# Residual stack on one core: the last projection's sums move from GpSimd to VectorE and to adding DMAs, its products add up in the PSUM bank

## The chip, the core and the metric

One core of a Trainium2 chip runs the whole program. Its engines are TensorE (PE in the profile, with its weight loads as PEld), VectorE (DVE), ScalarE (ACT), GpSimd (POOL) and SyncE (SP), which issues DMAs. Sixteen DMA engines move data between DRAM and the on-chip memory. The metric is the device time of one execution in microseconds; lower is better.

## The reference, cut to what matters

There are four residual layers on `x`, of 64 x 32 rows (2048) by 512 columns:

```python
x = x + L0(x)    # per-batch 32 x 32 mixing of the rows of a batch
x = x + L1(x)    # 512 x 512 linear layer plus a rank-16 adapter
x = x + L2(x)    # attention with a paged cache: 32 query heads, 8 key heads, head size 128
x = x + L3(x)    # per-batch 32 x 32 mixing, as in L0, with other weights
```

What the change touches is the end of L2, and L3. The heads' outputs `o` (2048 x 4096) are multiplied by `Wo` (4096 x 512) and added to `x`; then L3 takes, for each batch of 32 rows, `out = x + W_b^T x`. Everything is 32-bit floating point.

## The kernel before, in words

**Stages.** The first three layers up to the attention fill most of the time. They write `x` after L1 into 16 DRAM tiles `x_dram[t]` of 128 rows, and the turned head outputs into `o_dram[g][t]`: for each tile t of 128 rows and each half g of the key heads, 128 x 16 x 128 numbers. The last stage (from L1483 on) multiplies `o` by `Wo`, adds, mixes and stores.

**Two levels of Strassen's scheme (in Winograd's form).** The rows are cut into four quads q of four tiles. One quad is a 2 x 2 block matrix: i chooses two of its tiles, j chooses the half g of the heads. `Wo` is likewise cut into 2 x 2 blocks: heads by columns `lo` and `hi`. Seven products, numbered 1 to 7, give the quad's four blocks of the result. Each of them is one `Outer(what, quad)`, and `TARGETS` (L1505) says into which result blocks its output goes: 14 additions of a 128 x 512 block for a quad. Within an Outer the same scheme is used again: operand tiles "11", "12", "21", "22" of 128 x 1024, sums s1 to s4 of them, and seven products p of eight 128 x 128 x 128 matmuls each (`ORDER`, L290). I call one such product a **step**. `Outer.multiply` (L342) issues its matmuls into a bank of PSUM, `Outer.post` (L358) reads the bank.

**What an Outer costs each engine before.** The operand tiles come from `o_dram` by SP's DMAs into a ring of 12 tiles of 512 KB (`ring_tile`, L280; `load`, L309; `release`, L322). VectorE makes s1 to s4 (L340). For Outers 7, 5, 6 and 3 the operands are themselves sums of blocks: `combine` (L1575) makes them, on VectorE for 7, 6 and the first 5, on GpSimd for the others. Each product has a bank of its own out of six; ScalarE copies the first into `u` (L362), and VectorE adds the later ones to it and to one another: seven adds from a bank for an Outer (L367 to L380). The result `m` of 128 x 512 is then added by GpSimd into `acc` (L1519), which holds the rows of a quad on chip; `acc` has two buffers, so quads are loaded (L1499) and stored (L1503) between their two rounds.

**The weights' sums.** For each of the seven numbers, `weight_sum` (L246) makes four sums of blocks of `Wo`, in two halves of 128 x 512 each (L251). Before, in the last stage, GpSimd makes those for 2 (the fourth), 7, 4, 6 and 3, VectorE those for 5. `first_weights` (L1559) and `second_weights` (L1563) are VectorE's.

**L3.** `fetch_mix` (L1521) gathers 32 weights for each row by an indirect DMA from GpSimd, `make_diag` (L1526) spreads them on VectorE into a block-diagonal 128 x 128 matrix, and `mixed` (L1536) multiplies it with the rows on TensorE, adds the product to the rows on VectorE (L1544) and may send the part out; `store_out` (L1548) sends a tile.

**Order.** Everything in this stage is issued in an order written out by hand; each engine works through its own queue in that order. Outers 1 of quads 0 and 1 have been made during the end of the attention, from GpSimd's loads. `order` (L1590) then has 26 Outers: first round 2, 2, 7, 7, 4, 4 of quads 0 and 1, and 1, 7, 2, 4 of quads 2 and 3; second round 5, 6, 3 of quads 3, 0, 1, 2. The loop at L1726 takes steps 0 to 181. After each step's matmuls and its `post` come releases, then what `then(step, ...)` has put under this step, then `pump` (L1583), which issues waiting loads of `o` on SP as far as ring tiles are free. So a number given to `then` decides both when work is issued and what it stands behind on its engine. An offset like `s - 4` is four steps before the Outer's first.

Of the kernel before, what the change touches and what calls it, by code (L numbers as in the profile page):

```python
# [77 lines left out]
def resid_kernel(  # L78
# [128 lines left out]
    x_dram = [dram.tile([P, HID], F32, name=f"x_{t}") for t in range(NT)]  # L207
# [38 lines left out]
    def weight_sum(what, name, engine):  # L246

        w = w_of[what]
        a, b = {1: ("3", "11"), 2: ("22", "1"), 3: ("22", "3"), 4: ("2", "21")}[name]
        for k in (0, 1):  # L250
            engine.tensor_tensor(w.part(str(name), k), w.part(a, k), w.part(b, k), ALU.subtract)  # L251
# [6 lines left out]
    def fourth_weights(k, i, engine):  # L258

        lo, hi = slice(0, HID // 2), slice(HID // 2, HID)  # L260
        dst = w_sb["o", KG + k][:, :, hi]
        if i == 0:
            engine.tensor_tensor(dst, w_sb["o", k][:, :, hi], w_sb["o", k][:, :, lo], ALU.add)
        else:
            engine.tensor_tensor(dst, dst, w_sb["o", KG + k][:, :, lo], ALU.subtract)
# [19 lines left out]
    class Outer:  # L285
# [13 lines left out]
        FROM = {1: (0, 0), 2: (0, 1), 4: (1, 1)}  # L299
        count = 0  # L300

        def __init__(self, what, quad):
            self.what, self.quad = what, quad
            self.m, self.tag = {}, {}
            self.n = Outer.count
            Outer.count += 1
            self.pair = 0 if self.n < 3 else self.n % 2

        def load(self, key, queue=nc.sync, block=None):  # L309
            i, j = block or self.FROM[self.what]  # L310
            a, b = int(key[0]) - 1, int(key[1]) - 1
            self.tag[key], self.m[key] = ring_tile()
            queue.dma_start(
                out=self.m[key],
                in_=o_dram[j][4 * self.quad + 2 * i + a][:, b * 2 * REP : (b + 1) * 2 * REP],
            )

        def adopt(self, key, other):

            self.tag[key], self.m[key] = other.tag.pop(key), other.m.pop(key)  # L320
# [33 lines left out]

        def block(self, a, h):
            return self.out[:, a, h * P : (h + 1) * P]

        def post(self, p):  # L358
# [20 lines left out]
            else:  # L379
                add(self.block(1, 0), self.u3, ps, ALU.subtract)  # L380
# [1102 lines left out]
    with ExitStack() as l3:  # L1483
# [10 lines left out]
        acc, diag, rows_of_mix = {}, {}, {}  # L1494

        def load_rows(q):
            acc[q] = pool.tile([P, 4, HID], F32, name="acc", bufs=2)
            for a in range(4):
                nc.sync.dma_start(out=acc[q][:, a], in_=x_dram[4 * q + a])  # L1499

        def store_rows(q):
            for a in range(4):
                nc.scalar.dma_start(out=x_dram[4 * q + a], in_=acc[q][:, a])  # L1503
# [11 lines left out]
        def accumulate(o, engine):  # L1515
            op = ALU.subtract if o.what == 4 else ALU.add
            for i, j in TARGETS[o.what]:
                part = acc[o.quad][:, 2 * i : 2 * i + 2, (lo, hi)[j]]
                engine.tensor_tensor(part, part, o.out, op)  # L1519

        def fetch_mix(q, a):  # L1521
            t = 4 * q + a
            rows_of_mix[t] = pool.tile([P, S], F32, name="mix_rows")
            gather(rows_of_mix[t], w3, cond_rows[:, t : t + 1])

        def make_diag(q, a):  # L1526
            t = 4 * q + a
            diag[t] = pool.tile([P, NB, S], F32, name="mix_diag", bufs=4)
            add(  # L1529
                diag[t],  # L1530
                rows_of_mix.pop(t).unsqueeze(1).to_broadcast([P, NB, S]),
# [4 lines left out]
        def mixed(q, a, cols, queue=nc.scalar):  # L1536
# [3 lines left out]
            part = acc[q][:, a, cols]  # L1540
# [3 lines left out]
            add(part, ps, part, ALU.add)  # L1544
# [3 lines left out]
        def store_out(q, a, queue=nc.scalar):  # L1548
            t = 4 * q + a
            queue.dma_start(out=out[t * P : (t + 1) * P, :], in_=acc[q][:, a])  # L1550
# [16 lines left out]
        class Operand:  # L1567


            load, release = Outer.load, Outer.release  # L1570

# [3 lines left out]
        def combine(dst, key, a, op, b, engine):  # L1575
            engine.tensor_tensor(dst.m[key], a.m[key], b.m[key], op)  # L1576
# [12 lines left out]
        with tc.manual_schedule(engines=ENGINES):  # L1589
            order = [(2, 0), (2, 1), (7, 0), (7, 1), (4, 0), (4, 1)]  # L1590
            order += [(w, q) for q in (2, 3) for w in (1, 7, 2, 4)]
            order += [(w, q) for q in (3, 0, 1, 2) for w in (5, 6, 3)]
# [3 lines left out]
            KEYS = ("21", "22", "11", "12")  # L1596

            for what, q in order[1:]:
                o, s = of[what, q], base[what, q]
                begin = {"s1": -2, "s2": -2, "s3": -1, "s4": 1}  # L1600
                if what in (1, 2, 4):
                    for key in ("11", "12", "21", "22"):
                        pending.append((o, key, None))
                if what == 7:
                    single = (1, q) not in of
                    a11 = Operand(q) if single else of[1, q]
                    for key in KEYS:
                        if single:
                            pending.append((a11, key, (0, 0)))
                        pending.append((o, key, (1, 0)))  # L1610
                    when = (-5, -4, -4, -3) if single else (-9, -6, -6, -9)
                    for key, w in zip(KEYS, when):
                        then(s + w, combine, o, key, a11, ALU.subtract, o, nc.vector)
                        if single:
                            then(s + w, a11.release, key)
                if what == 1:
                    begin["s3"] = 0
                if what == 5:
                    a22 = Operand(q)
                    for key in KEYS:  # L1620
                        pending.append((o, key, (1, 0)))
                        pending.append((a22, key, (1, 1)))
                    for key in ("21", "12", "11", "22"):
                        pending.append((of[6, q], key, (0, 0)))
                    for key in ("21", "12", "11", "22"):
                        pending.append((of[3, q], key, (0, 1)))
                    first = q == 3
                    engine = nc.vector if first else nc.gpsimd
                    for key, w in zip(KEYS, (-10, -8, -5, -4) if first else (-11, -9, -7, -5)):
                        then(s + w, combine, o, key, o, ALU.add, a22, engine)  # L1630
                        then(s + w, a22.release, key)
                    for key, w in zip(("21", "12", "11", "22"), (-1, -1, 1, 2)):
                        then(s + w, combine, of[6, q], key, o, ALU.subtract, of[6, q], nc.vector)
                    for key, w in zip(("21", "12", "11", "22"), (4, 5, 6, 7)):
                        then(s + w, combine, of[3, q], key, of[3, q], ALU.subtract, of[6, q], nc.gpsimd)
                    begin["s3"] = 0
                for name, w in begin.items():
                    then(s + w, o.sum, name, nc.vector)
                then(s + 6, accumulate, o, nc.gpsimd)
            then(6, accumulate, early[2], nc.gpsimd)  # L1640

            for w, what, name in (
                (0, 7, 1),
                (1, 7, 2),
                (3, 7, 4),
                (5, 7, 3),
                (9, 4, 1),
                (11, 4, 2),
                (13, 4, 4),
                (15, 4, 3),  # L1650
            ):
                then(w, weight_sum, what, name, nc.gpsimd)
            for q, w in ((0, 37), (1, 44), (2, 73)):
                then(w, store_rows, q)
            then(39, load_rows, 2)
            then(50, load_rows, 3)
# [4 lines left out]
            for k in range(KG):  # L1661
                then(s + 18, first_weights, k)
                then(s + 25, second_weights, k)
            for w, what, name in (
                (20, 5, 1),
                (21, 5, 2),
                (22, 5, 4),
                (26, 5, 3),
                (27, 6, 1),
                (28, 6, 2),  # L1670
                (29, 6, 4),
                (30, 6, 3),
                (33, 3, 1),
                (34, 3, 2),
                (36, 3, 4),
                (38, 3, 3),
            ):
                engine = nc.vector if what == 5 else nc.gpsimd
                then(s + w, weight_sum, what, name, engine)
            for q in (3, 0, 1, 2):  # L1680
                s = base[3, q]
                for a in range(4):
                    then(s - 14 + 3 * a, fetch_mix, q, a)
                    then(s - 12 + 3 * a, make_diag, q, a)
                if q != 2:
                    for a in range(4):
                        then(s + 10 + a, mixed, q, a, slice(0, HID), None)
                        then(s + 11 + a, store_out, q, a)
            for q, w in ((0, 80), (1, 130), (2, 151)):
                then(w, load_rows, q)  # L1690
            s = base[3, 2]
            todo[s + 6] = [x for x in todo[s + 6] if x[0] is not accumulate]
            then(s + 1, mixed, 2, 2, slice(0, HID), nc.sync)
            then(s + 2, mixed, 2, 3, slice(0, HID), nc.sync)
            then(s + 3, mixed, 2, 0, lo, nc.sync)
            then(s + 4, mixed, 2, 1, lo, nc.sync)
            last = outers[-1]

            def part_of_last(a, h):
                at = HID // 2 + h * P  # L1700
                return acc[2][:, a, at : at + P]

            def add_to_last(a, h, b):
                add(part_of_last(a, h), part_of_last(a, h), b, ALU.add)

            then(s + 2, lambda: add_to_last(0, 0, last.block(0, 0)))
            then(s + 3, lambda: add_to_last(1, 0, last.u3))
# [123 lines left out]
```

## Time and profile before

| | us |
|---|---|
| median of 3 runs (lowest, highest) | 2493.77 (2492.73, 2495.66) |
| the profiled execution, its own time | 2495.89 |
| its span in the trace | 2494.1 |
| busy in the span: PE, DVE, POOL, ACT | 2391.5, 1847.8, 1472.3, 1404.3 |
| last stage, PE's first product to the end of the span | 2056.6 to 2494.1 |
| POOL in the last stage: adds into acc, combinations | 101.4, 65.3 |

Lines of the profile name an engine, a line of the kernel, an operation, what it writes and reads, and a count. "<-" after an idle time names what ended it. One 128 x 128 x 128 matmul is recorded twice, so a step has 16 records. A window's line gives its length, then the busy time and records of each engine, the clock granted to TensorE, the busy share of the 16 DMA engines and what they moved in GB/s. Times of single instructions within the text are microseconds from the span's start.

### The profile page before, as it was taken

What the parts mean: (1) busy time and instruction counts of PE and PEld (TensorE: products, weight loads), DVE (VectorE), ACT (ScalarE), POOL (GpSimd) and SP (SyncE); (2) the same over time, 40 slices, a digit from 0 to 9 for tenths busy, and PEclk for the clock granted to TensorE, in tenths of its full rate; (3) what the DMA queues carried; (4) which work ended last, traced back from release to release, by engine and by line L of the source; (5) the groups of instructions that cost most, each with busy time, mean ns of one, the idle gap of its engine ahead of it and who ended that gap; (6) DMA issues with size and microseconds to landing.
All of it is one profiled execution on the core that took longest, in us unless ns stands there. A gap on an engine that the chain in (4) does not pass through costs nothing. (4 is left out here: it accounts for less than half of the span.)

```text
span 2494.1 us, 50604 instructions
## 1 busy us (share of the span) xinstructions
PE 2391.5 (96%) x15142; PEld 1896.7 (76%) x15142; DVE 1847.8 (74%) x3788; ACT 1404.3 (56%) x4024; POOL 1472.3 (59%) x1394
## 2 busy tenths in 40 slices
PE   8999999999999999999999999999999897996787
PEld 4657777777777777777777777777777797996787
DVE  5567777777777777887877777777777777668766
ACT  2347777777777777676777777777777650000000
POOL 3346565656566666665565666566566658226774
PEclk9999999999999999999999999999999999998999
DMA  8876767676667677766666666666578767774552
GB/s 274 259 228 183 207 183 208 184 202 190 196 191 203 188 229 238 214 187 183 180 175 194 175 192 173 194 177 188 174 220 249 226 197 288 240 275 140 168 210 83
DMA packets 485696, 502.66 MB, mean 202 GB/s; under 512 B 69952, under 2 KB 392768, under 8 KB 485424
## 3 DMA queue, kind: packets, MB, share of 16 engines
q1 hardware_dynamic: 425552, 311.00, 40.8%
q0 software_dynamic: 55600, 181.35, 24.7%
q10 hardware_dynamic: 4272, 7.08, 0.8%
q8 instruction: 122, 2.00, 0.3%
q14 instruction: 150, 1.23, 0.2%
HBM read 427.91 MB, written 79.69 MB: 204 GB/s over the span
## 5 line engine op out<-in xcount | busy, mean ns | idle before, releaser
L105 POOL DMA_INDIRECT v_sb<-v,v_rows x512 | 546.3, 1067 | 354.0 <-PE o_ps L1055 243.3
L1055 PE MATMUL o_ps<-pT,v_sb 128*128 128x128 f32 x4096 | 624.9, 275 | 1.1 <-ACT oT L1090 0.8
L1055 PEld LDWEIGHTS o_ps<-pT,v_sb 128*128 128x128 f32 x4096 | 578.3, 191 | 28.9 <-ACT oT L1090 1.4
L1022 ACT ACTIVATE sm<-sm,top 128x544 f32<-128x544 f32 x512 | 380.9, 744 | 341.4 <-DVE top L1011 252.0
L1011 DVE CUSTOM_DVE_ANT_0 sm<-s_ps,pen 128x544 f32<-128x544 f32 x512 | 369.1, 721 | 102.9 <-PE s_ps L1006 83.7
L1028 ACT ACTIVATE sm<-sm,share 128x512 f32<-128x512 f32 x512 | 369.8, 722 | 101.8 <-DVE share L1027 64.5
L1047 DVE COPY pT<-pT_ps 128x512 f32<-128x512 f32 x512 | 353.0, 689 | 56.5 <-PE pT_ps L1045 15.3
L1003 PE MATMUL s_ps<-kT,qT 128*128 128x288 f32 x1024 | 335.2, 409 | 3.1 <-issue 2.7
L831 DVE TENSOR_TENSOR raw<-proj_ps,raw 128x512 f32<-128x512 f32 x332 | 224.3, 687 | 131.5 <-PE proj_ps L819 117.0
L1045 PE MATMUL pT_ps<-ident,sm 128*128 128x128 f32 x2048 | 309.8, 274 | 4.8 <-ACT qT L933 3.8
L1006 PE MATMUL s_ps<-kT,qT 128*128 128x256 f32 x1024 | 305.7, 380 | 2.1 <-ACT p_new L1029 1.1
L974 POOL TENSOR_SCALAR pen<-key_f,seq_f 128x544 f32<-128x544 f32 x128 | 283.2, 2213 | 13.5 <-DMA kT<-kT 2.2
L1003 PEld LDWEIGHTS s_ps<-kT,qT 128*128 128x128 f32 x1024 | 177.9, 191 | 147.6 <-issue 131.8
L1045 PEld LDWEIGHTS pT_ps<-ident,sm 128*128 128x128 f32 x2048 | 239.1, 142 | 8.8 <-ACT qT L933 4.8
L875 ACT ACTIVATE sq<-raw 128x128 f32<-128x128 f32 x640 | 198.4, 310 | 73.7 <-DVE raw L831 56.3
L1006 PEld LDWEIGHTS s_ps<-kT,qT 128*128 128x128 f32 x1024 | 194.9, 191 | 57.0 <-issue 1.7
L362 ACT COPY u<-out_ps 128x128 f32<-128x128 f32 x26 | 6.9, 266 | 403.9 <-PE out_ps L347 260.5
L347 PE MATMUL out_ps<-wo,o_in 128*128 128x128 f32 x1664 | 204.7, 281 | 21.2 <-DVE o_in L340 14.6
L880 POOL TENSOR_SCALAR ss<-ss 128x4 f32<-128x4 f32 x160 | 38.4, 240 | 310.2 <-ACT sq L875 304.4
L347 PEld LDWEIGHTS out_ps<-wo,o_in 128*128 128x128 f32 x1664 | 197.5, 197 | 29.2 <-DVE o_in L340 14.2
L1027 DVE RECIPROCAL share<-total 128x1 f32<-128x1 f32 x512 | 83.9, 164 | 179.7 <-ACT sm L1022 151.0
L1519 POOL TENSOR_TENSOR acc<-acc,m 128x512 f32<-128x512 f32 x55 | 101.4, 1865 | 146.9 <-DVE m L380 146.9
(209 smaller groups left out, 3963.0 us busy)
## 6 DMA issues: line engine op xcount, KB each, us to landing
kT<-kT SPq DMA_DIRECT2D x2048, 64.0 KB
o_in<-o SPq DMA_DIRECT2D x124, 512.0 KB
o<-oT POOLq DMA_DIRECT2D x68, 256.0 KB
o<-oT SPq DMA_DIRECT2D x58, 256.0 KB
v<-in_kv_cache SPq DMA_DIRECT2D x32, 256.0 KB
kT<-page_rows SPq DMA_DIRECT2D x32, 256.0 KB
vn<-raw SPq DMA_DIRECT2D x32, 256.0 KB
v_sb<-v,v_rows POOLq DMA_INDIRECT x512
```

The lines of the kernel that those rows point to most:

```text
L105: nc.gpsimd.indirect_dma_start(out=dst, out_offset=None, in_=table, in_offset=bass.IndirectOffsetOnAxis(ap=index, axis=0),)
L347: nc.tensor.matmul(self.ps, lhsT=self.m[o][:, i, :], rhs=w_of[self.what].part(w, i // REP)[:, i % REP, :], start=(i == 0), stop=(i == 2 * ...
L831: nc.vector.tensor_tensor(dst, self.ps.rearrange("p (h d) -> p h d", h=REP), src, ALU.add)
L974: nc.gpsimd.tensor_scalar(self.pen, key_f, seq_f[:, self.b : self.b + 1], BIG, ALU.is_ge, ALU.mult)
L1003: nc.tensor.matmul(ps[:, first:HID], lhsT=q, rhs=self.kT[:, :n1, k, :], start=True, stop=True)
L1006: nc.tensor.matmul(ps[:, HID : first + LA], lhsT=q, rhs=self.kT[:, n1:, k, :], start=True, stop=True)
L1011: nc.vector.tensor_tensor_reduce(out=sm, in0=ps[:, first : first + LA], in1=self.pen, scale=1.0, scalar=3e38, op0=ALU.add, op1=ALU.min, ac ...
L1022: nc.scalar.activation(sm, sm, AF.Exp, bias=top, scale=-1.0, accum_out=total)
L1028: nc.scalar.activation(sm[:, :L], sm[:, :L], AF.Copy, scale=share)
L1045: nc.tensor.transpose(ps[:, c, :], self.sm[k][:, c * P : (c + 1) * P], ident)
L1047: nc.vector.tensor_copy(pT, ps)
L1055: nc.tensor.matmul(o_of[self.s, k][:, self.j, :], lhsT=self.v[c][:, k * D : (k + 1) * D], rhs=self.pT[k][:, c, :], start=(self.j == 0 and ...
```

## The change

The function's calls outside the last stage keep their work; only signs are turned (`weight_sum` 4, `fourth_weights`), so that every product is added and none subtracted. In the last stage:

1. **x stays in DRAM.** `accumulate` sends each Outer's result to DRAM by DMAs from GpSimd's queue that add onto `x` there (`accum_op=ALU.add`), one for each target block (256 KB). There is no `acc`; the rows of a quad are loaded once, after its last Outer, from GpSimd's queue, and the last Outer of all is added on chip by VectorE.
2. **GpSimd makes no sums.** The weights' sums and the combinations go to VectorE. For 5, the second block is loaded onto the first by an adding DMA (`load_onto`). The second sum, the operand of 6, is made in the first round, when the blocks of 7 and 4 are on chip (`second_sum`), stored to DRAM (`s2_dram`) from one of two tiles, and loaded for 6 in the second round.
3. **Products add up in the bank.** The products are taken in the order `LATER`, and an Outer uses three banks: 0 takes four products one after the other, with a copy by ScalarE after each; 1 takes one; 2 takes two. VectorE has three adds of 128 x 128 for an Outer, two of them from a bank, ScalarE four copies. Tiles "11", "21" and "12" are released one product later.
4. **L3.** The identity is added to the gathered weights (one more VectorE add of 128 x 32 for each tile), so the matmul gives `x + W^T x`, and ScalarE copies it. Results of quads 0 to 2 are stored from GpSimd's queue.
5. **Order.** The second round takes the quads 0, 1, 2, 3; the weights' sums and the sums' steps are placed anew. The load of the operands of 4 of quad 0 comes ahead of that of 7 of quad 1.

```diff
+        LATER = (0, 1, 2, 5, 3, 4, 6)
...
+            if self.what == 6:
+                queue.dma_start(out=self.m[key], in_=s2_dram[self.quad, key])
...
+        def load_onto(self, key, block):
+            nc.gpsimd.dma_start(
+                out=self.m[key], in_=self.source(key, block), accum_op=ALU.add
             )
...
+        def multiply_later(self, p, chunks, bank):
+            if p < 2 or p == 3:
+                if chunks[0] == 0:
+                    self.banks[(0, 1, None, 2)[p]] = bank()[:, :P]
+            ps = self.banks[(0, 1, 0, 2, 0, 2, 0)[p]]
+            o, w = self.ORDER[self.LATER[p]]
+            for i in chunks:
+                nc.tensor.matmul(
+                    ps,
+                    lhsT=self.m[o][:, i, :],
+                    rhs=w_of[self.what].part(w, i // REP)[:, i % REP, :],
+                    start=(i == 0 and p in (0, 1, 3)),
+                    stop=(i == 2 * REP - 1),
+                    skip_group_check=True,
+                )
+        def post_later(self, p):
+            add, copy = nc.vector.tensor_tensor, nc.scalar.copy
+            if p == 0:
...
+                copy(self.block(0, 0), self.banks[0])
+            elif p == 1:
+                add(self.block(0, 0), self.banks[1], self.block(0, 0), ALU.add)
+            elif p == 2:
+                copy(self.block(0, 1), self.banks[0])
+            elif p == 3:
+                self.u = o_pools[0].tile([P, P], F32, name="u1")
+                copy(self.u, self.banks[2])
+            elif p == 4:
+                copy(self.block(1, 1), self.banks[0])
+            elif p == 5:
+                add(self.block(1, 1), self.block(1, 1), self.u, ALU.add)
+                add(self.block(0, 1), self.banks[2], self.block(0, 1), ALU.add)
+            else:
+                copy(self.block(1, 0), self.banks[0])
...
-        def accumulate(o, engine):
-            op = ALU.subtract if o.what == 4 else ALU.add
+        def accumulate(o):
             for i, j in TARGETS[o.what]:
-                part = acc[o.quad][:, 2 * i : 2 * i + 2, (lo, hi)[j]]
-                engine.tensor_tensor(part, part, o.out, op)
+                x = x_pair[2 * o.quad + i].rearrange("a p c -> p a c")
+                nc.gpsimd.dma_start(out=x[:, :, (lo, hi)[j]], in_=o.out, accum_op=ALU.add)
...
-            add(part, ps, part, ALU.add)
+            nc.scalar.copy(part, ps)
...
+        def second_sum(q, key):
+            s2 = pool.tile([P, 2 * REP, P], F32, name="s2_out", bufs=2)
+            add(s2, of[4, q].m[key], of[7, q].m[key], ALU.subtract)
+            nc.gpsimd.dma_start(out=s2_dram[q, key], in_=s2)
+        def fourth_sum(q, key):
+            o = of[3, q]
+            add(o.m[key], o.m[key], of[6, q].m[key], ALU.subtract)
...
-            order += [(w, q) for q in (3, 0, 1, 2) for w in (5, 6, 3)]
+            order += [(w, q) for q in range(4) for w in (5, 6, 3)]
...
+                    for key, w in zip(KEYS, (-10, -8, -6, -5)):
+                        then(s + w, o.load_onto, key, (1, 1))
+                    for key, w in zip(KEYS, (3, 6, 4, 5)):
+                        then(s + w, fourth_sum, q, key)
...
-                engine = nc.vector if what == 5 else nc.gpsimd
-                then(s + w, weight_sum, what, name, engine)
+                then(s + w, weight_sum, what, name, nc.vector)
...
+                s = base[3, q] - (9 if q == 3 else 0)
                 for a in range(4):
-                    then(s - 14 + 3 * a, fetch_mix, q, a)
-                    then(s - 12 + 3 * a, make_diag, q, a)
+                    then(s + 4 + 2 * a, fetch_mix, q, a)
+                    then(s + 6 + 2 * a, make_diag, q, a)
+                if q < 3:
+                    for i in (0, 1):
+                        then(s + 7, load_rows, q, i)
                     for a in range(4):
-                        then(s + 10 + a, mixed, q, a, slice(0, HID), None)
-                        then(s + 11 + a, store_out, q, a)
+                        then(s + 13 + a, mixed, q, a, slice(0, HID), None)
+                        then(s + 14 + a, store_out, q, a)
```

## The prediction

> **What bounds the kernel now.** The page's 40 slices show PE at 9 tenths or more nearly everywhere, but at 6, 7, 8, 7 in the last four; every line of the diff that changes work sits in that last stage, so I cut it out. The timeline of PE gives the first product of each Outer; the windows between those starts are, in order: (2,0) to (7,1); (4,0) to (4,3), ten Outers; then 5, 6, 3 of quad 3; of quad 0; of quad 1; of quad 2 with the tail. Columns: length, busy time of PE, PEld, DVE, ACT, POOL, granted clock, DMA share, GB/s.
>
> ```profile
> 2056.60:2125.30 68.70, 55.15 (x449) 52.76 (x450) 48.05 (x49) 1.06 (x4) 57.05 (x38) 0.98 0.77 283
> 2125.30:2257.90 132.60, 127.37 (x1122) 126.94 (x1121) 93.22 (x133) 2.65 (x10) 34.43 (x19) 0.99 0.77 257
> 2257.90:2330.50 72.60, 44.89 (x338) 43.83 (x337) 54.10 (x48) 0.80 (x3) 58.96 (x34) 0.81 0.32 112
> 2330.50:2381.70 51.20, 44.32 (x347) 41.45 (x346) 36.72 (x46) 0.80 (x3) 35.30 (x18) 0.93 0.60 206
> 2381.70:2432.90 51.20, 44.26 (x347) 41.39 (x346) 35.49 (x46) 0.80 (x3) 35.29 (x18) 0.93 0.61 208
> 2432.90:2494.10 61.20, 48.72 (x360) 43.80 (x358) 38.42 (x57) 0.80 (x3) 26.00 (x14) 0.92 0.23 80
> ```
>
> An undisturbed product (a step) takes 1.787 us: in the timeline seven of them run from 2137.77 to 2150.28. 182 steps are 325.2 us, and 16 mixing matmuls of 0.86 us add 13.8: a floor of 339.0. The stage takes 434.7 (2056.6 to PE's last instruction, which ends at 2491.3). So 95.7 us are excess. By window, length less 28, 70, 21, 21, 21, 21 steps and the mixing in it: 18.7, 7.5, 35.1, 10.2, 10.2, 14.0. The waits of PE and of DVE in the stage say who makes it (us in total, times, longest):
>
> ```profile
> PE out_ps L347 <- DVE s L340: 41.7, 11, 12.1
> PE out_ps L347 <- DVE o_in L340: 14.6, 13, 4.9
> PE mix_ps L1541 <- POOL acc L1519: 7.1, 1, 7.1
> ```
> ```profile
> DVE mix_diag L1529 <- DMA mix_rows<-in_w,cond_rows: 35.9, 11, 6.6
> ```
>
> PE waits for DVE's sums. DVE in turn is held twice by POOL: its gathers stand late in POOL's queue, and its own adds stretch while POOL reads. In the timeline of DVE, the same add of 128x1024 that takes 1.2 us alone:
>
> ```profile
> 2240.96 1.21 DVE L340 TENSOR_TENSOR s<-o_in 128x1024 f32<-128x1024 f32 x1
> ...
> 2282.44 11.02 DVE L340 TENSOR_TENSOR s<-o_in 128x1024 f32<-128x1024 f32 x1
> ...
> 2311.03 5.60 DVE L1529 TENSOR_TENSOR mix_diag<-mix_rows,same 128x128 f32<-128x128 f32 x1 [2.09 <-DMA mix_rows<-in_w,cond_rows]
> ```
>
> The 11.02 us cover POOL's adds from 2283.0 to 2292.4, and PE waits 12.08 behind it. A long wait costs more than itself: after it the 16 records of a step take 3.75 us instead of 1.95 (2294.87), with the granted clock at 0.81 in that window.
>
> **GpSimd's work.** Removed from POOL in the stage, by its groups: 55 adds into acc (101.4 us), 28 combinations (65.3), 34 halves of weight sums (60.5): 227 of 247 us. None was on PE's path by its own length, but for the 7.1 above; their worth is what they did to DVE.
>
> **DVE's work, after**, at undisturbed durations (median 1.216 for 128x1024, 0.68 for 128x512, 0.285 for an add from a bank): 104 operand sums and 48 combinations (16 each of third, second, fourth) are 152 x 1.22 = 185; 8 first and second weights 9.8; 42 halves of weight sums 28.6; 3 posts in place of 7 on 26 Outers 22.2; 16 diagonals with an added 0.19 us add 7.7. Together 254 us against 306 busy before, though it takes over nearly all that POOL did. By window, against the floor: first 33 x 1.22 + 18 x 0.68 + 12 x 0.285 = 56 of 50; second 91 of 125; third 34 of 37.5, after a crowded end of the second; the others 24 of 41. So DVE is over the floor in the first window alone, and nearly full in the third.
>
> **ScalarE** gets 4 copies of 0.266 us per Outer and 16 of 0.58 (its 128x512 copy from a bank, 0.579): 37 us in 378, beside PE. The new wait, PE's third product on ScalarE's copy of the first out of the same bank, has one step (1.79 us) of cover against 0.27. An Outer takes 3 of 6 banks instead of 7, so a late DVE no longer holds PE through banks. Tiles are released one product later, so a load starts 1.8 us later; the 12-tile ring covers that except in the first window.
>
> **DMA.** Copies: 108 loads of o instead of 124 (0.524 MB each, 56.6 MB), 16 stores of the second sum 8.4, weights 6.3, rows in 4.2, results 4.2: 79.7 MB. Adding: 16 onto o tiles 8.4 MB and 55 onto x 14.4 MB: 22.8 MB. Removed: 28 loads of acc, 12 stores. The rate comes from the queue rows of this stage (packets, MB, share of 16 engines in 438 us):
>
> ```profile
> q1 hardware_dynamic: 29232, 79.70, 52.8%
> ```
>
> 79.70 / (0.528 x 438) = 345 GB/s. So the copies take 231 us of all 16 engines. No adding DMA is in the trace. It cannot cost less than a copy of its bytes (66 us), and not more than three copies (199): a load of the one operand, of the other, and a store. I take 1.5 copies, since it reads twice and writes once where a copy reads once and writes once: 99, together 330 us. That is 87% of a 378 us stage, under the 0.94 that the window 2225 to 2260 held. Ends: 297 and 430.
>
> The Trainium skill speaks against this choice: "Collectives: The Full Stack", section "The bandwidth ceiling: the fold count and why AG ≠ RS ≠ AR", has a reducing transfer run at about half the rate of a copying one, because both sources go through the same read ring. No run here shows it yet. By it the adding would be 132 us, the total 363, and at 0.94 the stage would take 386, 8 us more than my sum.
>
> **POOL's queue after** holds 107 plain or adding issues at about 0.58 us (its own o_in issues, 0.583) and 16 gathers (18.7): some 80 us, perhaps 140 if an adding issue costs double; either fits. What counts is its new waits. Each add onto x waits for its Outer's last copy; the rows of a quad wait until the last add has landed. Behind that wait stand two gathers, and for those DVE's diagonals. PE mixes 7 steps (12.5 us) after the last Outer of the quad ends, and in this time an add and a load must land. A gather's landing takes 2.3 to 6.4 us in the chain of waits; two of those fit barely. The second sum has two tiles, so DVE waits about 3 us per quad for a store; outside the first window it has that time.
>
> **The sum, excess before to after.** First window 18.7 to 14: the pool's tiles still open at about 2062.5 (SP's and POOL's first issues in the timeline), then some 55 us of DVE follow; the 3.9 us in which SP issues eight acc loads ahead of o are gone. Second 7.5 to 4. Third 35.1 to 7: stretched adds, late gathers and cold clock go, a nearly full DVE stays. Quads 0 and 1, 10.2 to 4 each. Last 14.0 to 6: the 7.1 goes, the wait for rows remains. 39 us in all instead of 95.7: 57 us less. The early stages stay. Span 2494.1 - 57 = 2437.1, and with the 1.8 us that lie around the span 2438.9; that execution took 2495.9, which is 2.1 above the median of 2493.8, so against the median the forecast is **2437**. Bounds of the forecast's own case: excess 15 (all stalls but the start's) gives 2413; at 2 copies with some idle queue, 2455.
>
> **Rivals.**
> DMA becomes the bound, still faster: 2 to 2.7 copies make 363 to 410 us of DMA, over 0.94 a stage of 386 to 435: 2445 to 2493. For it: 0.94 in one window already, and bursts at the first window. Against: 0.23 to 0.61 in the last three.
> Slower, by the adding DMAs on all 16 engines: from 2.7 copies on (231 + 2.7 x 66 = 409, over 0.94 = 435) the stage is longer than today's; at three copies it takes 458, and the execution 2517. For it: the adds onto x move 1 KB runs, and each must read DRAM before it writes. Against: three separate copies would also move the data through buffers, which this does not.
> POOL's queue in place of POOL's arithmetic: rows land 5 us too late in each of four quads, and DVE keeps half of its 35.9 us of gather waits; about 20 us of the gain go: 2457.
> The change doesn't do what it says: PE's waits for s in the third window come from DVE's own amount of work, and DVE takes on more. Then only the 7.1 and part of the first window go, and the rest is exchanged: 2490. Against: 254 is less than 306.
>
> **Chances.** Forecast's case (2413 to 2455) 0.62; DMA-bound but faster 0.14; POOL's queue 0.08; exchanged, within 0.2% (5 us, about what a measurement of this kernel can tell from no change) 0.03; slower 0.13. Faster 0.84. The range takes the first case, POOL's queue and the greater part of the DMA-bound one: 2412 to 2484.
>
> **What the changed profile would show.** Right: no sum on POOL; DVE's s at 1.22 us with none over 2; PE's waits on s under 10 us; the third window near 45 us and the quads at 43 to 46, at a clock of 1.0; DMA share 0.8 to 0.9. Wrong: waits of PE's mixing on rows or of DVE on gathers or second-sum stores over 5 us per quad (POOL's queue); loads of o as PE's releaser with DMA shares over 0.95, and q0's share far above its megabytes (adding dearer than 1.5 copies). The forecast fails if an adding DMA costs over 2 copies, or if the first window grows.

## The result and the profile after

The changed kernel takes 2510.53 us (median of 4 runs, 2509.20 to 2511.72) where the kernel before takes 2493.47 beside it (2492.73 to 2495.66). The ratio is 1.0067, 95% interval 1.0049 to 1.0084: **slower**, by 17 us or 0.7%, where the forecast was 57 us faster. The profiled execution took 2510.93 us, its span is 2509.2.

The windows of the last stage, cut at the same places as before ((2,0) to (7,1); (4,0) to (4,3); 5, 6, 3 of each quad; the columns are the same, and the quads now come as 0, 1, 2, 3):

```profile
2060.90:2145.60 84.70, 59.21 (x448) 58.15 (x449) 50.58 (x65) 5.17 (x20) 16.32 (x24) 0.84 0.86 274
2145.60:2303.00 157.40, 130.38 (x1122) 129.87 (x1121) 78.19 (x91) 13.58 (x51) 30.95 (x31) 0.91 0.84 224
2303.00:2354.90 51.90, 40.52 (x336) 39.53 (x336) 38.78 (x52) 3.99 (x15) 14.77 (x13) 0.96 0.99 256
2354.90:2405.40 50.50, 44.24 (x344) 41.84 (x344) 22.80 (x33) 6.34 (x19) 19.37 (x20) 0.91 0.95 246
2405.40:2455.10 49.70, 43.03 (x344) 40.73 (x344) 22.66 (x33) 6.34 (x19) 19.60 (x20) 0.95 0.95 246
2455.10:2509.20 54.10, 48.07 (x356) 43.36 (x356) 24.11 (x44) 8.74 (x24) 17.87 (x19) 0.94 0.52 127
```

Two different things are to be seen. The first round (two windows) is 41 us longer than before: 242.1 for 201.3. The second round is 30 us shorter, most of it in the third window (51.9 for 72.6). With the 4.3 us by which the stage begins later, that makes the 15 us by which this span is longer. So the change did part of what the forecast said, and paid for it elsewhere. DVE's busy time, the fourth column, fell as forecast: 237 us in the stage (forecast 254, before 306). It isn't DVE's work that made the first round long, since DVE is busy 129 of 242 us there. ScalarE makes five copies for an Outer, not the four of the text on the change and of the prediction (the fifth takes the first product of bank 2 into `u`); it is busy 44 us in the stage, not 37, and still far from full.

TensorE's waits in the stage, and then VectorE's (us in total, times, longest):

```profile
PE out_ps L374 <- DVE o_in L351: 44.0, 6, 14.9
PE out_ps L374 <- DMA o_in<-o: 21.1, 5, 6.5
```
```profile
DVE s_out L1638 <- issue: 30.5, 3, 14.0
...
DVE mix_rows L1578 <- DMA mix_rows<-in_w,cond_rows: 25.2, 9, 5.0
```

Before, TensorE waited 41.7 us for DVE's `s`, 33.7 of them in the second round. Now it waits 44.0 for the sums s3 and s4 (written over `o_in`), 41.0 of them in four places of the first round. And DVE itself is idle 30.5 us ahead of `s_out`, the tile of the second sum (another 2.4 are put down to its store). DVE's largest wait in the stage, 57.6 us for a copy by ScalarE (L398), is one for TensorE, on whose product that copy waits; in the kernel with the banks alone, which is faster than before, it is 40.4. One place of the waits for `s_out`, in DVE's timeline and then in GpSimd's (a DMA's time is that of its issue):

```profile
2184.18 2.35 DVE L1638 TENSOR_TENSOR s_out<-o_in 128x1024 f32<-128x1024 f32 x2
2195.79 1.23 DVE L1638 TENSOR_TENSOR s_out<-o_in 128x1024 f32<-128x1024 f32 x1 [9.26 <-issue]
```
```profile
2183.92 4.84 POOL L1567 DMA_DIRECT2D x<-m  x4 [11.32 <-ACT m L403]
2187.22 2.67 POOL L1639 DMA_DIRECT2D s<-s_out  x2
2197.31 0.54 POOL L1639 DMA_DIRECT2D s<-s_out  x1 [7.42 <-DVE m L391]
```

Read together: GpSimd issues four adds onto x (1 MB), and right behind them the stores of the first two second sums of quad 2. Both of the tiles are then taken. The profile names no releaser here ("issue"). That the third sum waits for the landing of the first store follows from the two tiles, and the DMA packets fit: on GpSimd's queue those of the adds (1 KB) start until 2194, those of the stores (4 KB) only from 2192.5 on. DVE goes on at 2195.8, which is 8.6 us after GpSimd began to issue that store. Behind the third sum on DVE stand s3 and s4 of the Outer that TensorE is at (2198.26, 2199.40), so TensorE stands still too: 9.15 us at 2199.62. The two queues of the stage:

```profile
q1 hardware_dynamic: 22464, 63.58, 42.0%
q0 software_dynamic: 21424, 38.81, 41.2%
```

q0 is GpSimd's. In a window of 453 us it takes 187 us of the 16 engines for 38.8 MB, q1 190 us for 63.6 MB: per byte q0 is 1.6 times as dear, and about 22 of its 38.8 MB are added. This counts the time of packets, as the shares do.

### The profile page after: what moved, and what is told of

It is laid out like the page before. It is cut to its first block, busy times and chain, and to the rows that moved or that the text cites. A ratio compares the mean times of both kernels' runs of the same rounds, so it can differ in the third digit from the quotient of the medians.

```text
span 2509.2 us, 50637 instructions
## 1 busy us (share of the span) xinstructions
PE 2394.7 (95%) x15140; PEld 1902.8 (76%) x15140; DVE 1778.1 (71%) x3730; ACT 1439.7 (57%) x4146; POOL 1348.3 (54%) x1384
## 3 DMA queue, kind: packets, MB, share of 16 engines
q1 hardware_dynamic: 418784, 294.88, 38.8%
## 4 chain that ended last, share of the span: by engine, by line
PE 82%; DMA 8%; DVE 3%; issue 2%; SPq 2%; ACT 1%; POOL 1%; ACTq 0%; DVEq 0%; POOLq 0%
PE proj_ps L869 22%; PE o_ps L1105 16%; PE s_ps L1053 9%; PE out_ps L374 9%; PE pT_ps L1095 8%; PE s_ps L1056 8%; PE head_ps L971 3%; PE l_ps L686 3%; DMA o_in<-o 2%; DMA s<-s_out 1%; PE o_ps L1118 1%; SPq L1009 1%; DMA kT<-kT 1%; DMA wo<-in_wo 1%; PE s_ps L1088 1%
## 5 line engine op out<-in xcount | busy, mean ns | idle before, releaser
L374 PE MATMUL out_ps<-wo,o_in 128*128 128x128 f32 x1664 | 215.2, 291 | 70.5 <-DVE o_in L351 44.0
L374 PEld LDWEIGHTS out_ps<-wo,o_in 128*128 128x128 f32 x1664 | 208.6, 206 | 76.8 <-issue 46.9
L869 PE MATMUL proj_ps<-sum,x 128*128 128x512 f32 x380 | 188.0, 597 | 0.0
L1567 POOL DMA_DIRECT2D x<-m x55 | 67.9, 1547 | 221.4 <-ACT m L403 166.8
```

The costliest lines, as they stand in the source:

```text
L374: nc.tensor.matmul(ps, lhsT=self.m[o][:, i, :], rhs=w_of[self.what].part(w, i // REP)[:, i % REP, :], start=(i == 0 and p in (0, 1, 3)), s ...
L869: nc.tensor.matmul(self.ps, lhsT=self.pair.x[x][:, c if x == "b" else half.start + c, :], rhs=blocks(self.b)[w][:, c, :], start=(c == 0), ...
```

## The experiments

Theory A: the stores of second sums stand behind adding DMAs, two tiles are too few, and DVE stops. Theory B: the DMA engines have more to move than the stage allows. Theory C: VectorE has too much work. Times are medians; "before" is its median in the same comparison.

**Four tiles for the second sum**

```diff
-            s2 = pool.tile([P, 2 * REP, P], F32, name="s2_out", bufs=2)
+            if turn < 2:
+                s2 = pool.tile([P, 2 * REP, P], F32, name="s2_out", bufs=2)
+            else:
+                s2 = spare[:, turn - 2]
```

> The second sum gets four tiles in place of two (two of them are halves of the tile that holds a quad's rows later). Theory A (in the first round VectorE stops because each third second sum must wait until the first one's store has landed, and the stores stand in GpSimd's queue behind adding DMAs): VectorE's waits on the second sum's tiles (32.9 us) go to under 5, TensorE's waits of 5 to 15 us on operand sums in the first round go, and the kernel takes 25 to 35 us less than the changed one: 2476 to 2486. Theory B (the 16 DMA engines have more to move than the stage allows, so any wait that goes comes back as a wait for loads): within 5 us of 2510. Theory C (VectorE has too much of its own work since GpSimd's sums went to it): within 5 us of 2510, with VectorE busy without gaps in the first round.

Measured: 2480.58 (before 2492.41; ratio 0.9949, 0.9930 to 0.9968). DVE has no wait on `s_out` left. TensorE's waits for sums, 44.0 us for `o_in` and 4.8 for `s`, are now 11.1 and 12.4:

```profile
PE out_ps L374 <- DMA o_in<-o: 20.5, 5, 7.0
PE out_ps L374 <- DVE s L351: 12.4, 4, 5.3
PE out_ps L374 <- DVE o_in L351: 11.1, 3, 4.9
```

Theory A holds, and B and C in the form that allows no gain fall: with every adding DMA and all of VectorE's sums in place, 30 us come back from two more tiles. The first line shows what stays: the loads of 5 in the second round (21.1 us before).

**The stores on ScalarE's queue**

```diff
-            nc.gpsimd.dma_start(out=s2_dram[q, key], in_=s2)
+            nc.scalar.dma_start(out=s2_dram[q, key], in_=s2)
```

> Two tiles as in the changed kernel, but the second sum is stored from ScalarE's queue, so that no adding DMA stands ahead of it in its queue. Theory A: a store of 0.5 MB lands 2 to 4 us after it is issued, VectorE's waits on the second sum's tiles fall from 32.9 us to under 12, and the kernel takes 20 to 30 us less than the changed one: 2480 to 2490. A part may come back, since ScalarE's copies out of the bank now stand behind a store that waits for VectorE. Theory B (DMA engines full): the stores land as late as before, within 5 us of 2510.

Measured: 2498.60 (before 2492.41; 1.0027, 1.0015 to 1.0038). That is 12 us less than the changed kernel, half of what was expected. DVE's waits in the first round:

```profile
DVE s_out L1638 <- DMA s<-s_out: 18.1, 5, 6.9
...
DVE s_out L1638 <- issue: 5.2, 1, 5.2
```

They fell from 32.9 to 23.3 us, not under 12. A store in another queue has no adding DMA ahead of it there, but uses the same 16 engines, and DVE still waits up to 6.9 us. In addition ScalarE stood 41.1 us in five waits for a second sum whose store was next in its queue, and TensorE's waits for its copies rose from 4.0 to 9.4 us. So the place in the queue is a part of the lateness only; with four tiles DVE no longer waits for it.

**The early results' adds later**

```diff
             eye = pool.tile([P, S], F32, name="eye")
+            nc.gpsimd.memset(eye, 0.0)
             for e in (0, 1):
                 accumulate(early[e])
```

> The adding DMAs of the two results that the attention's end makes stand behind a write into the last stage's own memory on GpSimd, so they can start only once the attention's memory is free. Theory (those DMAs delay the attention's own gathers): the last stage's first product comes at 2056 to 2058 as before the change and not at 2060.9, and the kernel takes 3 to 4 us less than the changed one, 2506 to 2508, or up to 4 more if 2 MB of adding now stand ahead of the first second-sum stores. Rival (the attention's end is later for another reason, such as turned signs or where code lies): first product at 2060 to 2061.

Measured: 2513.46 (before 2492.41; 1.0078, 1.0060 to 1.0096), no gain. The stage's first product did come at 2055.91, but (4,0) began 91.6 us later instead of 84.8, so the 2 MB of adds cost as much there. The 4.3 us by which the stage began later in the changed kernel are also partly chance: in the five profiled runs with these adds in the attention's end it begins between 2053.9 and 2060.9 (mean 2058.0), in the seven without them between 2054.0 and 2056.6 (mean 2055.6). Some 2 us may be theirs.

**Stores onto x without adding**

```diff
-                nc.gpsimd.dma_start(out=x[:, :, (lo, hi)[j]], in_=o.out, accum_op=ALU.add)
+                nc.gpsimd.dma_start(out=x[:, :, (lo, hi)[j]], in_=o.out)
```

> The 55 DMAs onto x write without adding (this leaves out the additions onto x; bytes, queue, waits and number of DMAs stay). If an adding DMA takes the engines about 2.1 times as long as a copy (worked out from the two queues' shares), the 14.4 MB cost 43 us instead of 91, the stores behind them land earlier, and the kernel takes 25 to 45 us less than the changed one: 2465 to 2485, GpSimd's queue share of the stage falling from 41% to about 31%. If adding costs what a copy does, within 4 us of 2510 and the same share.

Measured: 2477.62 (before 2492.41; 0.9931, 0.9913 to 0.9948), 33 us less. q0's share of the stage:

```profile
q0 software_dynamic: 11616, 38.74, 29.5%
```

29.5% of 421 us are 124 us of the engines in place of 187: the 13.4 MB of adds in this window took 63 us more than as plain stores. The run changes more than the addition, though. The packets under 2 KB, first in the changed kernel and then here:

```profile
DMA packets 44209, 103.24 MB, mean 227 GB/s; under 512 B 3984, under 2 KB 23824, under 8 KB 44176
DMA packets 34394, 103.14 MB, mean 245 GB/s; under 512 B 3984, under 2 KB 10768, under 8 KB 34362
```

The adds go as 13056 packets of 1 KB, which took 97 us of the 16 engines; the plain stores go as packets of 4 KB and took about 34. That is 2.8 copies, and no run tells what the addition and what the smaller packets cost (in the changed kernel's stage plain packets of 1 KB on q1 took 53 ns each, those of the adds 117). DVE's longest wait on `s_out` fell from 14.0 to 9.1, and the quads took 46.6 and 46.1 us in place of 50.5 and 49.7. So the two causes act together: dear adds make the stores late, and two tiles let DVE feel it.

**The parts of the change one by one, onto the kernel before.** First GpSimd's sums given to VectorE (`nc.gpsimd` to `nc.vector` in eight calls, nothing else):

```diff
-                then(s + 6, accumulate, o, nc.gpsimd)
+                then(s + 6, accumulate, o, nc.vector)
...
-                engine = nc.vector if what == 5 else nc.gpsimd
+                engine = nc.vector
```

> The kernel before, with one part of the change alone: the 55 adds into acc, the 28 combinations and the 34 halves of weight sums that GpSimd made in the last stage are made by VectorE at the same places of the order. VectorE's work at undisturbed durations becomes 253 + 92 = 345 us (55 x 0.68, 28 x 1.22, 34 x 0.68 more). Theory (GpSimd's arithmetic costs TensorE time through VectorE's stretched adds and late gathers): 15 to 40 us less than before, 2453 to 2478, most of it in the second round. Rival (VectorE has no room; what GpSimd did is only exchanged): 2485 to 2500, with TensorE waiting for VectorE through the banks.

Measured: 2448.51 (before 2495.63; 0.9815, 0.9799 to 0.9832), 47 us faster, a little more than the theory's range. The third window and two quads, before 72.6 and 51.2:

```profile
2253.50:2307.80 54.30, 44.12 (x339) 42.49 (x338) 51.88 (x80) 0.80 (x3) 4.75 (x4) 0.87 0.50 174
2307.80:2352.80 45.00, 42.03 (x347) 39.35 (x346) 39.29 (x60) 0.80 (x3) 5.67 (x4) 1.00 0.71 236
2352.80:2397.10 44.30, 42.00 (x347) 39.32 (x346) 39.34 (x60) 0.80 (x3) 5.74 (x4) 1.00 0.71 241
```

VectorE does all of the sums and is busy 319 us, hardly more than the 306 before: GpSimd's 227 us of arithmetic became 13 us on VectorE, since its own adds no longer stretch. One of their groups before and here, where the mean falls from 2305 to 1215 ns:

```profile
L340 DVE TENSOR_TENSOR s<-o_in 128x1024 f32<-128x1024 f32 x25 | 57.6, 2305 | 8.2 <-DMA o_in<-o 8.2
L340 DVE TENSOR_TENSOR s<-o_in 128x1024 f32<-128x1024 f32 x26 | 31.6, 1215 | 0.0
```

The clock in the quads is 1.00, before 0.93.

Then the products in the bank alone, and both together:

> The kernel before, with another part alone: products add up in three banks, ScalarE makes four copies and VectorE three adds for an Outer; GpSimd keeps its sums. Theory (this part is harmless and relieves VectorE by some 30 us): 0 to 15 us less than before, 2478 to 2493, with GpSimd's stretch in the third window still there. Rival (a product must wait for ScalarE's copy of the one before in its bank, and later releases hold loads): 5 to 20 us more than before, 2498 to 2513.

> The kernel before with both parts: no arithmetic on GpSimd, sums in the banks, but acc stays on chip, the second sum is made in the second round as before, and no DMA adds. VectorE's work becomes some 345 - 30 = 315 us of a stage of about 390. Theory (the change's two arithmetic parts bring what was forecast and its adding DMAs and stored second sums take it away again): 30 to 50 us less than before, 2443 to 2463. Rival (arithmetic on VectorE brings nothing by itself): 2480 or more.

Measured: the banks alone 2482.38 (before 2495.63; 0.9953, 0.9936 to 0.9969), 13 us faster, with the stretch still there (TensorE waits 38.1 us for `s`); both 2438.40 (0.9775, 0.9759 to 0.9792), 57 us faster, more than the 30 to 50 expected. No DMA adds in that kernel and the second sum is made in the second round.

**Backwards from the changed kernel.** The second sum is made in the second round, in place:

```diff
-            s2 = pool.tile([P, 2 * REP, P], F32, name="s2_out", bufs=2)
-            add(s2, of[4, q].m[key], of[7, q].m[key], ALU.subtract)
-            nc.gpsimd.dma_start(out=s2_dram[q, key], in_=s2)
+            o = of[6, q]
+            add(o.m[key], of[5, q].m[key], o.m[key], ALU.subtract)
```

> The changed kernel with the second sum made in the second round again, in place from a loaded block, as before the change: no stores of it (8.4 MB less), as many adds on VectorE, the additions by DMA onto x and onto the o tiles stay. Theory A (the first round is held by stores of second sums behind adding DMAs with two tiles): the first round, from the stage's first product to the first product of 5, takes 200 to 215 us in place of 244, the second stays within 5 us, and the kernel takes 30 to 45 us less than the changed one: 2465 to 2480. Theory B (the DMA engines are full in any case): 25 us of transfers go and 10 to 25 us of time, spread over both rounds: 2485 to 2500.

Measured: 2471.20 (before 2495.63; 0.9914, 0.9893 to 0.9934), 39 us less than the changed kernel. The first round takes 198 us, not 242 (measured from the stage's first product to that of 5): shorter than the kernel before's. The quads stay at 50.2 and 49.2. That is theory A, in size and in place.

Then, in addition, a tile of its own for the second block of 5, and with that the adds onto x as plain stores:

```diff
-                        then(s + w, o.load_onto, key, (1, 1))
+                        then(s + w, load_other, q, key)
+                        then(s + v, first_sum, q, key)
```

> As the run with the second sum back in the second round, and in addition the second block of 5 is loaded into a tile of its own (two of them, from GpSimd's queue) and added by VectorE, so only the additions onto x are left to DMAs. Theory (an adding load stands behind the adds onto x and can start only when the plain load has landed, and TensorE waits for it, 22 us in that run): these waits fall under 8 us, and the kernel takes 5 to 15 us less than that run's 2471: 2456 to 2466. What then remains above the 2438 of the run with all sums on VectorE and none by DMA, 18 to 28 us, is the price of the adds onto x. Rival (16 more adds on VectorE, 5 us per quad, take back what goes): 2468 to 2478.

> As the run with the second sum back and the second block of 5 in tiles of its own, but the DMAs onto x write without adding (this leaves out the additions onto x). It asks what the 26 us are by which that run lies above the one with all sums on VectorE (2464 against 2438). Theory (the price of adding: under load the adds onto x take the 16 engines about 2.5 times a copy, 63 us more than plain stores): 12 to 22 us less, 2442 to 2452. Rival (the order of waits: rows are loaded only after the last result of a quad, and gathers stand behind that on GpSimd): within 4 us of 2464.

Measured: 2464.20 (before 2493.21; 0.9893, 0.9870 to 0.9916) and 2443.81 (before 2495.52; 0.9796, 0.9779 to 0.9812). In the first the 22 us of TensorE's waits for landing loads are gone, but the time fell by 7 us with intervals that overlap, so what the adding loads cost is not settled (VectorE now waits 36.4 us for the second blocks of 5). The second gives back 20 of the 26 us that were in question. q0 in the stage, with adds and without:

```profile
q0 software_dynamic: 19120, 30.42, 36.5%
```
```profile
q0 software_dynamic: 9312, 30.35, 21.5%
```

36.5% of 402 us less 21.5% of 386 are 64 us, the same difference as in the other pair.

**The disputed price by itself.** Four groups of DMAs behind the end of the kernel with both arithmetic parts, in one run; beside the first group the last 0.39 MB of results still move, otherwise nothing else does:

```diff
+            for op in (ALU.bypass, ALU.add):
+                for i in range(16):
+                    to = goal[i // 2].rearrange("a p c -> p a c")[:, :, (lo, hi)[i % 2]]
...
+                wait_for(goal[7][1][:, HID - S :])
```

> The run with both arithmetic parts, and after its end four groups of DMAs from GpSimd's queue alone, each waited for: 16 stores of 128x2x256 (4.19 MB, runs of 1 KB) to DRAM, the same 16 with adding, 8 loads of 128x1024 (4.19 MB) into tiles, the same 8 with adding. At the 334 GB/s of the changed kernel's copies a group of copies takes 12.6 us plus some 2 us to the first landing. If adding costs 1.5 copies as predicted, the adding groups take 19 to 22 us; if 2.1 (from the queues' shares), 27 to 30; from the run with plain stores onto x, the adds onto x should be the dearer ones, 33 to 36 us, and the adding loads 16 to 20.

GpSimd's timeline: issues of 16 stores and the wait for the last; the same with adding; 8 loads and the copy that waits for them; the same with adding.

```profile
2430.22 11.59 POOL L1801 DMA_DIRECT2D goal<-acc  x16 [2.17 <-DVE m L390]
2447.33 0.58 POOL L1791 DMA_DIRECT2D mix_rows<-goal  x1 [5.52 <-DMA goal<-acc]
...
2449.50 19.83 POOL L1799 DMA_DIRECT2D goal<-acc  x16
2475.89 0.60 POOL L1791 DMA_DIRECT2D mix_rows<-goal  x1 [6.57 <-DMA goal<-acc]
...
2478.38 4.27 POOL L1810 DMA_DIRECT2D o_in<-o  x8 [0.30 <-issue]
2492.81 0.21 POOL L1811 COPY mix_rows<-o_in 128x32 f32<-128x32 f32 x1 [10.16 <-DMA o_in<-o]
2493.25 7.10 POOL L1808 DMA_DIRECT2D o_in<-o  x8 [0.23 <-issue]
2516.38 0.21 POOL L1811 COPY mix_rows<-o_in 128x32 f32<-128x32 f32 x1 [16.03 <-DMA o_in<-o]
```

4.19 MB each: stores 17.1 us, adding stores 26.4; loads 14.4, adding loads 23.1. That is 1.54 and 1.60 copies from first issue to last landing. Within a group the rates were 311 and 190 GB/s (16 of the 311 are the last results), 387 and 209: adding runs at 0.64 and 0.54 of a copy. In time of packets, the unit of the queue rows, adding is dearer. The stores and the adding stores:

```profile
q0 software_dynamic: 1280, 4.20, 74.8%
q0 software_dynamic: 4352, 4.20, 106.5%
```

74.8% of 17.1 us are 12.8 us of the 16 engines, 106.5% of 26.4 are 28.1: 2.2 copies. For the loads, 82.6% of 14.4 and 94.4% of 23.1 make 1.8. (A share over 100% means that packets on one engine overlap, so this unit counts more than the engine's time.) The expectation that adds onto x are much dearer than adding loads falls. And the stage's other traffic isn't what makes them dear: a 1 KB packet of an add took 108 ns alone and 117 in the changed kernel's stage, 13.4 MB at the price measured alone would be 90 us, and they took 97.

**A version that beats both.** Both arithmetic parts, gathers four steps earlier into four tiles, and the weights' sum for 2 behind two operand sums:

```diff
-            rows_of_mix[t] = pool.tile([P, S], F32, name="mix_rows")
+            rows_of_mix[t] = pool.tile([P, S], F32, name="mix_rows", bufs=4)
...
-                    then(s - 14 + 3 * a, fetch_mix, q, a)
+                    then(s - 18 + 3 * a, fetch_mix, q, a)
```

> The kernel before with both arithmetic parts (2438), and the mixing weights gathered four steps earlier into four tiles in place of one, and the weights' sum for 2 made behind the first two operand sums. Theory (VectorE's idle 7.0 us for a gather in the third window, with TensorE's 6.4 us behind it, is only that gather's lateness): 5 to 9 us less, 2429 to 2434. Rival (VectorE has more work than time in that window, 50.7 us busy of 59.6, and something else is late next): 2436 to 2440.

Measured: 2430.57 (before 2493.21; 0.9742, 0.9729 to 0.9755). Its third window and the next quad:

```profile
2246.90:2298.40 51.50, 40.85 (x338) 39.70 (x338) 50.49 (x69) 3.98 (x15) 7.89 (x4) 0.97 0.53 180
2298.40:2339.40 41.00, 41.00 (x347) 39.09 (x346) 36.79 (x48) 3.98 (x15) 5.46 (x4) 1.00 0.75 259
```

The third window fell from 59.6 to 51.5 us, and DVE is busy 50.5 of them: there its own work is the bound now. In the quad TensorE is never idle.

## Why the prediction was wrong

Against the kernel before, in the same comparisons, the parts add up like this:

| kernel | us against before |
|---|---|
| sums on VectorE | -47 |
| and products in the bank | -57 |
| and x by adding DMAs (rows loaded last, mixed with the identity, quads in the order 0 to 3) | -29; with plain stores onto x -52 |
| and the second block of 5 by an adding load | -24 |
| and the second sum stored in the first round: the change | +17 |

**What bounds the kernel, and what GpSimd's arithmetic cost: right.** DVE's stretched adds and late gathers held TensorE. With the sums moved the quads take 44 to 45 us (forecast 45), and with the banks 42 to 43. The kernel with both arithmetic parts is 57 us faster than before; the forecast for the whole change was 57. That the two numbers agree is partly luck: in that kernel the third window takes 59.6 us where some 45 were forecast, and the other windows less than forecast. What the prediction left for the stored second sum and the adding DMAs to cost was nearly nothing, and that is the error.

**The step that failed: "The second sum has two tiles, so DVE waits about 3 us per quad for a store; outside the first window it has that time."** DVE waited 32.9 us in five waits, up to 14.0, and behind the waiting sum stand s3 and s4, for which TensorE waits at once. The price of the part is 41 us by the table; four tiles give back 30 of them, and the other 11 no run separates. The prediction shows no row for its 3 us and doesn't ask what stands ahead of the stores: in the two longest waits (9.3 and 14.0 us, quads 2 and 3) four adds of an Outer 1 do, in the same queue. DVE's free time in a window doesn't help an instruction that stands at the head of its queue.

**The second step: adding at 1.5 copies.** From issue to landing 1.54 and 1.60 were measured alone. But the prediction's sum is one of packet time on the 16 engines, since its 345 GB/s and its limit of 0.94 come from those shares, and in this unit adding takes 2.2 copies for the stores and 1.8 for the loads, alone too. In the stage the adds onto x took 97 us for 13.4 MB, where 1.5 copies at 345 GB/s are 58. All queues together took 378 us of the engines (42.0, 41.2 and 0.2% of 453) where 330 were forecast. The Trainium skill, "Collectives: The Full Stack", section "The bandwidth ceiling: the fold count and why AG ≠ RS ≠ AR", has reducing run at about half the rate of copying, for collectives between several ranks. The 0.64 and 0.54 measured alone are near to that. The prediction's second sum by it, an estimate of 363 us, is nearer to the 378 than its own 330.

**"87% of a 378 us stage, under the 0.94" was the wrong test.** A mean share under a limit says nothing about the instants when a store must land. In the first round the share was 0.84 to 0.86 and the stores were late; TensorE waited for loads themselves only ahead of the 5 of each quad (21.1 us, 17.9 of them in the windows at 0.95 to 0.99).

**"The early stages stay": nearly.** Adds of the early results went in among the attention's gathers: some 2 us at most can be put down to that.

**The rivals.** Slower came true, but not by the mechanism given for it: with the adds as dear as they are, four tiles make the kernel faster than before (0.9949). DMA-bound but faster comes nearest to that kernel, at 2480.6, where loads are the longest wait. POOL's queue did cost, through stores instead of rows: TensorE's mixing waited under 1 us in all, DVE's gathers 25.2 us (before 35.9, gone in the forecast). "Exchanged" falls: with all sums VectorE is busy 319 us instead of 306, and the kernel 47 us faster.

**The signs named for failure were the right ones:** waits on second-sum stores over 5 us, loads of `o` as TensorE's releaser with shares over 0.95, and q0 far above its megabytes. All three stand in the profile above, and the first window grew, which the prediction names as its failing.

The waits for the first result's tile (TensorE 4.0 us for ScalarE's copy in the first window, with 1.5 in the fastest kernel) weren't tried by themselves.

## What to carry to other kernels

A buffer that is filled by an engine and emptied by a DMA needs as many tiles as the DMA's landing takes in its real queue, with what is queued ahead of it at that moment; look at what stands behind the filling instruction before its wait is called covered. Ask of each part of a change what it is worth alone: here two parts were worth 57 us, and the three that moved work to the DMA engines took 74 us away. Moving arithmetic from GpSimd to a busier VectorE can be nearly free, if GpSimd's own work is what stretches VectorE's.

## What the runs showed of the hardware that was not expected

An adding DMA alone took 1.54 (stores) and 1.60 (loads) of a plain one's time from first issue to last landing, but 2.2 and 1.8 of its packets' time on the 16 engines. Onto runs of 1 KB the adds went as packets of 1 KB where plain stores went as packets of 4 KB; such a packet took 108 ns alone and 117 beside the stage's other traffic, so the price is hardly one of the traffic. GpSimd's 227 us of sums and VectorE's 306 became 319 us on VectorE alone, and the clock granted in the quads rose from 0.93 to 1.00 as TensorE's waits went.
